# Cross-attention on one core: seven products for the first batch's output too, sums in PSUM taken at every stage, and the second batch's x in three places

## The chip, the cores and the metric

The kernel runs on one core of one Trainium2 chip, in fp32 throughout. The metric is the device time of one execution in microseconds. The profile comes from one further execution of the same program.

## The reference

Two batches of 2048 tokens with 640 channels attend with 20 heads of 32 channels to 77 text rows and 77 image rows of a context of 154 rows. Text and image have keys, values and softmax of their own; the two results are added.

```python
q = _split_heads(hidden_states @ Wq.T, H)
k = _split_heads(text @ Wk.T, H)
v = _split_heads(text @ Wv.T, H)
out_text = _merge_heads(_attend(q, k, v, sm_scale))
k_ip = _split_heads(ip @ Wk_ip.T, H)
v_ip = _split_heads(ip @ Wv_ip.T, H)
out_ip = _merge_heads(_attend(q, k_ip, v_ip, sm_scale))
out = out_text + IP_SCALE * out_ip
out = out @ Wo.T + bo
return out + residual
```

Here `_attend` is softmax(q k^T / sqrt(32)) v, IP_SCALE is 1, and the residual is x itself. All matrices lie in memory with the contracted dimension first, and the output is written with channels first.

## The kernel before

**Tiles.** The 640 channels are 5 row blocks of 128 (index c, four heads each; `NC`). A batch's 2048 tokens are 4 blocks of 512 (`TB`, index i) and two halves of 1024 (`sub`). The work is cut into 20 steps u: step u is pair q = u // 2 of batch and row block, and half sub = u % 2. Steps 0 to 9 are the first batch, 10 to 19 the second; step 20 is what is left of the attention.

**One step.** TensorE (PE) forms scores for 8 token tiles of 128 x 4 heads x 154 keys in three groups of 3, 3 and 2 tiles. Each group goes through a fixed sequence, and each of its members has a letter in the written orders, with the group's number behind it:

- R, `scores` (L216): TensorE, 32-row matmuls, in one half (four) of the eight PSUM banks.
- K, `take` (L228): ScalarE (ACT) copies the four banks into `pb`.
- M, `maxima` (L237): VectorE (DVE).
- S, `subtract` (L242): GpSimd (POOL).
- E, `exponential` (L248): ScalarE.
- D, `sums` (L255) and the reciprocals (L257): VectorE.
- N, `normalise` (L262): GpSimd.
- T, `transpose` (L269): VectorE, 32x32 blocks in place.

`pb` has three zones: odd steps share one, even steps take turns with the other two. In every even step, AT (`attend`, L278) multiplies the finished probabilities of the pair before with v for both halves, and CA (`take_attention`, L302 and L306) copies the result to `aT` on ScalarE.

**What fills TensorE beside it.** Items F0, F1, ... of a step are projections that need one bank each, and C0, C1, ... are the copies or takes of their results. `items_of` lists them: queries q of one 512-token block two or one steps ahead (`queries`, L184, five matmuls of 512 columns), keys k and values v of a row block (`project_kv`, L138, eight matmuls of 154 columns), and output chunks o and p. A chunk o is one row block by 512 tokens of the first batch's output, five matmuls (`Out.step`, L328); `Out.store` (L338) adds bias and residual on VectorE and stores. A chunk p is the last row block of the second batch's output without its last contraction block.

**After step 20.** The rest of the second batch's output (4 row blocks by 4 token blocks, contraction over 4 blocks) goes by Strassen's seven products: `group` handles two row blocks by two token blocks at a time, with products of 2 x 2 blocks (`product`, L430, two matmuls of 512 columns each), and the fifth contraction block added by `last_chunk` (L438). VectorE adds each product from PSUM to one or two sums in `pb` (`add`, L450 to L454). GpSimd forms the sums of weight blocks (`sum_w`, L386) and of token blocks (`sum_a`, L408) after the last N of step 19.

**The order.** The schedule is manual. `ORDERS` holds for each kind of step the half of the banks that R0, R1, R2 and AT use, the bank of each item, and the order of the work on TensorE, ScalarE, VectorE and GpSimd; a letter with a minus belongs to the step before. For a step of the first batch it reads:

```python
"even": (
    "1000", "547",
    "R0 R1 F1 R2 F2 F0 AT",
    "K0 K1 C1 K2 E0 E1 C2 E2 C0 CA",
    "C0 M0 M1 T1- C2 T2- C1 M2 D0 D1 D2 T0",
    "S0 S1 S2 N0 N1 N2",
),
```

Each engine runs its list strictly in that order and waits by semaphores for what an instruction reads or overwrites.

**Transfers.** All but a few of the first loads are issued by SP, in one queue in the order in which the program writes them; an entry that waits holds those behind it. `load_w` brings slices of the key and value weights into free slots in `aT`, `load_wq` the query weights of a row block (three places), `spread_v` copies v of a pair in 16 small transfers to four row groups, and `load_x` brings x in slices of 128 x 512. All four blocks of x of one batch stay in `xs`; the second batch's slices replace them in steps 6 to 9. `wo` is loaded in the second half of step 9, into the tile that held the context, after a first quarter of v's copies; then come the first three residuals.

Of the kernel before, what the change touches and what calls it, by code (L numbers as in the profile page):

```python
# [19 lines left out]
def kernel(  # L20
# [44 lines left out]
    NV = B * NHB * NC  # L65
    OPEN = 4
    FETCH = 3
# [4 lines left out]
    rpool = ctx.enter_context(tc.tile_pool(name="rpool", bufs=5))  # L72
# [9 lines left out]
    aT = const.tile([P, (NC + 1) * NHB, TB], F32, name="aT")  # L82

# [15 lines left out]
        aT[:, ds((NC - 1) * NHB + 2 * n, 2), :]  # L99
        .rearrange("p s t -> p (s t)")  # L100
        .rearrange("p (k o) -> p k o", k=NCC)
        for n in range(4)
# [47 lines left out]

    def spread_v(q):

        for g in range(G):
            for r in range(G):
                nc.sync.dma_start(
                    out=v4s[q % 2][r * D : (r + 1) * D, g].rearrange("p k d -> p (k d)"),
                    in_=squares(q)[g * D : (g + 1) * D],
                )
            if (q, g) == (NC - 1, 0):
                nc.sync.dma_start(out=wo, in_=WoT.rearrange("(c p) o -> p c o", p=P))  # L160
                for o in outs[:FETCH]:
                    o.fetch()
# [4 lines left out]
    def load_x():  # L167

        if slices:
            b, i, k = slices.pop(0)  # L170
            nc.sync.dma_start(out=xs[i][:, k], in_=xT[ts(k, P), ds(b * S + i * TB, TB)])
# [9 lines left out]
    def queries(u, h, pq):  # L181
        q, _, _, sub = step_of(u)
        for k in range(NC):
            nc.tensor.matmul(  # L184
                pq,
                wqs[q % 3][:, k, :],
                xs[sub * NH + h][:, k, :],
                start=(k == 0),
                stop=(k == NC - 1),
            )  # L190
# [95 lines left out]
    def rows_of_attention(b, c):  # L286


        if b == 0:
            return aT[:, ts(c, NHB)]  # L290
        if c == 0:
            return aT[:, ts(NC, NHB)]
        return aT[:, c - 1 : NHB * NHB : NHB]

    def take_attention(q, pa):
        b, c = divmod(q, NC)
        assert b == 0 or finished >= c * NC
# [11 lines left out]
    class Out:  # L309


        def __init__(self, v):
            self.v, self.n = v, len(outs)
            outs.append(self)
            self.b, r = divmod(v, NHB * NC)
            self.i, self.o = divmod(r, NC)
            self.tok = ds(self.b * S + self.i * TB, TB)
            self.res = self.po = None
            self.k = 0

        def fetch(self):

            if self.res is None:
                self.res = rpool.tile([P, TB], F32, tag="res", name=f"res_{self.v}")
                nc.sync.dma_start(out=self.res, in_=xT[ts(self.o, P), self.tok])

        def step(self):
            nc.tensor.matmul(  # L328
                self.po,
                wo[:, self.k, ts(self.o, P)],  # L330
                rows_of_attention(self.b, self.k)[:, self.i],
                start=(self.k == 0),
                stop=(self.k == NC - 1),
            )
            self.k += 1

        def store(self):
            nc.vector.scalar_tensor_tensor(  # L338
                self.res, self.po, bo_sb[:, self.o : self.o + 1], self.res, ALU.add, ALU.add
            )  # L340
            nc.sync.dma_start(out=outT[ts(self.o, P), self.tok], in_=self.res)
            for o in outs[self.n + 1 : self.n + 1 + FETCH]:
                o.fetch()


    outs = []
    for v in range(NV // B):
        Out(v)
    for i in range(NHB):
        Out(NV // B + i * NC + NC - 1)  # L350
    finished = 0
# [4 lines left out]
    PAIRS = ((0, 1), (2, 3))  # L356


    w_sums = xs[0].rearrange("p k t -> p (k t)").rearrange("p (n o) -> p n o", o=P)
    pb_flat = pb.rearrange("p z n g l -> p (z n g l)")  # L360
    pb_tiles = pb_flat.rearrange("p (n t) -> p n t", t=TB)
    a_sums = {(0, 0): xs[1], (0, 1): xs[2], (1, 0): xs[3], (1, 1): pb_tiles[:, :NC]}
    SUMS = (1, 4, 3, 7, 6)
    WSUMS = (1, 2, 5, 6, 7)

    def w_of(m, op, kp):

        (o1, o2), (k1, k2) = PAIRS[op], PAIRS[kp]
        blocks = [[wo[:, k, ts(o, P)] for k in (k1, k2)] for o in (o1, o2)]
        if m == 3:  # L370
            return blocks[0][0]
        if m == 4:
            return blocks[1][1]
        return w_sums[:, (op * 2 + kp) * len(WSUMS) + WSUMS.index(m)]

    def sum_w(op, kp, m):
        (o1, o2), (k1, k2) = PAIRS[op], PAIRS[kp]
        (a11, a12), (a21, a22) = [[wo[:, k, ts(o, P)] for k in (k1, k2)] for o in (o1, o2)]
        x, y, f = {
            1: (a11, a22, ALU.add),  # L380
            2: (a21, a22, ALU.add),
            5: (a11, a12, ALU.add),
            6: (a21, a11, ALU.subtract),
            7: (a12, a22, ALU.subtract),
        }[m]
        nc.gpsimd.tensor_tensor(w_of(m, op, kp), x, y, f)  # L386

    def blocks_of(ip, kp):
        return [[rows_of_attention(B - 1, k)[:, i] for i in PAIRS[ip]] for k in PAIRS[kp]]

    def a_of(m, ip, kp):
        if m == 2:
            return blocks_of(ip, kp)[0][0]
        if m == 5:
            return blocks_of(ip, kp)[1][1]
        return a_sums[(ip, kp)][:, SUMS.index(m)]

    def sum_a(ip, m):
        for kp in range(2):
            (b11, b12), (b21, b22) = blocks_of(ip, kp)  # L400
            x, y, f = {
                1: (b11, b22, ALU.add),
                3: (b12, b22, ALU.subtract),
                4: (b21, b11, ALU.subtract),
                6: (b11, b12, ALU.add),
                7: (b21, b22, ALU.add),
            }[m]
            nc.gpsimd.tensor_tensor(a_of(m, ip, kp), x, y, f)  # L408

    w_list = [(op, kp, m) for op in range(2) for kp in range(2) for m in WSUMS]  # L410

    def fetch_group(ip, op):
        for o in (1, 0):
            for i in range(2):
                nc.sync.dma_start(
                    out=sum_tile(ip, op, o, i),
                    in_=xT[ts(PAIRS[op][o], P), ds(S + PAIRS[ip][i] * TB, TB)],
                )

    def sum_tile(ip, op, o, i):  # L420
        return pb_tiles[:, NC + ((ip * 2 + op) * 2 + o) * 2 + i]

    def group(ip, op, bank_of):


        def product(m):
            ps = bank_of()
            own = {7: (0, 0), 6: (1, 1)}.get(m)
            for kp in range(2):
                nc.tensor.matmul(  # L430
                    ps, w_of(m, op, kp), a_of(m, ip, kp), start=(kp == 0), stop=(kp == 1 and not own)
                )
            if own:
                last_chunk(ps, *own, False)
            return ps

# [185 lines left out]
    def items_of(u):  # L622
# [3 lines left out]
        if u == NU:  # L626
            return [("p",)]
# [229 lines left out]
```

## Time and profile before

| | before |
|---|---|
| median of 3 runs | 515.19 us (514.83 to 515.55) |
| the profiled execution | 515.92 us |
| its span, first to last instruction | 514.1 us |
| TensorE busy | 504.6 us |
| VectorE busy | 398.4 us |
| GpSimd busy | 383.6 us |
| ScalarE busy | 242.9 us |
| moved by DMA | 52.03 MB, mean 101 GB/s |

The profile lists matmuls (PE) and weight loads (PEld) apart. An fp32 matmul shows as two records of each. Matmuls are pipelined, so the mean duration of a record is longer than the distance between two, and the distance is what a row of records costs. "Waits" are put down to the work that ended last before them.

### The profile page before, as it was taken

What the parts mean: (1) busy time and instruction counts of PE and PEld (TensorE: products, weight loads), DVE (VectorE), ACT (ScalarE), POOL (GpSimd) and SP (SyncE); (2) the same over time, 40 slices, a digit from 0 to 9 for tenths busy, and PEclk for the clock granted to TensorE, in tenths of its full rate; (3) what the DMA queues carried; (4) which work ended last, traced back from release to release, by engine and by line L of the source; (5) the groups of instructions that cost most, each with busy time, mean ns of one, the idle gap of its engine ahead of it and who ended that gap; (6) DMA issues with size and microseconds to landing.
All of it is one profiled execution on the core that took longest, in us unless ns stands there. A gap on an engine that the chain in (4) does not pass through costs nothing.

```text
span 514.1 us, 9615 instructions
## 1 busy us (share of the span) xinstructions
PE 504.6 (98%) x3998; PEld 271.0 (53%) x3998; DVE 398.4 (77%) x331; ACT 242.9 (47%) x421; POOL 383.6 (75%) x166
## 2 busy tenths in 40 slices
PE   8999999999999999999999999999999999999997
PEld 5657567567467565554454455444444544444442
DVE  0079899998989987988985898699887997176554
ACT  1175667666666556673564446546552760100000
POOL 0079999998998997789897688587796899991000
PEclk9999999999999999999999999999999999999999
DMA  8984321242164256211411220140111306254422
GB/s 250 355 224 120 97 68 47 61 112 62 50 210 145 58 174 205 55 48 29 137 40 43 77 72 1 42 131 18 43 38 44 100 15 182 76 172 143 143 82 82
DMA packets 54795, 52.03 MB, mean 101 GB/s; under 512 B 5728, under 2 KB 38752, under 8 KB 54752
## 3 DMA queue, kind: packets, MB, share of 16 engines
q1 hardware_dynamic: 54032, 51.09, 33.0%
q8 instruction: 31, 0.51, 0.4%
q10 hardware_dynamic: 720, 0.33, 0.2%
q14 instruction: 12, 0.10, 0.1%
HBM read 37.64 MB, written 10.49 MB: 94 GB/s over the span
## 4 chain that ended last, share of the span: by engine, by line
PE 93%; DMA 3%; ACT 1%; SPq 1%; DVE 1%; issue 0%; ACTq 0%
PE bank L184 32%; PE bank L328 20%; PE bank L278 11%; PE bank L216 10%; PE bank L430 9%; PE bank L138 8%; PE bank L438 3%; DMA aT<-in_L_xattn_Wk_ip_dram 2%; DMA x<-in_x_dram 1%; DMA wq<-in_L_xattn_Wq_dram 1%; SPq L492 1%; ACT pb L248 1%; DVE den L255 0%; ACT aT L302 0%; ACT pb L228 0%
## 5 line engine op out<-in xcount | busy, mean ns | idle before, releaser
L242 POOL TENSOR_TENSOR pb<-pb,mx 128x1848 f32<-128x1848 f32 (+1 forms) x60 | 175.6, 2943 | 71.1 <-DVE mx L237 70.8
L262 POOL TENSOR_TENSOR pb<-pb,rden 128x1848 f32<-128x1848 f32 (+1 forms) x60 | 175.0, 2942 | 10.1 <-DVE rden L257 8.4
L184 PE MATMUL bank<-x,wq 128*128 128x512 f32 x400 | 180.5, 601 | 1.1 <-ACT pb L228 0.7
L237 DVE TENSOR_REDUCE mx<-pb 128x24 f32<-128x1848 f32 (+1 forms) x60 | 109.4, 1845 | 50.7 <-ACT pb L228 50.7
L228 ACT COPY pb<-bank 128x462 f32<-128x462 f32 (+1 forms) x240 | 101.1, 541 | 54.2 <-PE bank L216 52.9
L184 PEld LDWEIGHTS bank<-x,wq 128*128 128x128 f32 x400 | 73.8, 191 | 89.2 <-issue 79.7
L255 DVE TENSOR_REDUCE den<-pb 128x24 f32<-128x1848 f32 (+1 forms) x60 | 110.3, 1838 | 12.5 <-ACT pb L248 12.2
L248 ACT ACTIVATE pb<-pb 128x1848 f32<-128x1848 f32 (+1 forms) x60 | 94.9, 1583 | 51.0 <-POOL pb L242 50.9
L269 DVE STREAM_TRANSPOSE pb<-pb 128x1920 f32<-128x1920 f32 (+1 forms) x60 | 114.7, 1927 | 2.4 <-POOL pb L262 2.4
L328 PE MATMUL bank<-aT,wo_ct 128*128 128x512 f32 x240 | 107.4, 599 | 0.0
L328 PEld LDWEIGHTS bank<-aT,wo_ct 128*128 128x128 f32 x240 | 44.3, 190 | 55.8 <-issue 52.6
L216 PEld LDWEIGHTS bank<-kT,qT 32*128 32x128 f32 x1280 | 48.4, 184 | 32.9 <-issue 28.6
L216 PE MATMUL bank<-kT,qT 32*128 32x154 f32 x1280 | 59.4, 307 | 2.1 <-DVE res L338 0.7
L278 PE MATMUL bank<-pb,v 32*32 32x512 f32 x1600 | 55.7, 597 | 1.0 <-issue 1.0
L194 ACT COPY qT<-bank 128x512 f32<-128x512 f32 x40 | 22.9, 585 | 53.1 <-PE bank L184 53.1
L138 PEld LDWEIGHTS bank<-wo_ct,aT 128*128 128x128 f32 x320 | 43.2, 188 | 4.9 <-issue 3.4
L138 PE MATMUL bank<-wo_ct,aT 128*128 128x154 f32 x320 | 44.9, 295 | 0.5 <-DMA aT<-in_L_xattn_Wk_ip_dram 0.5
L278 PEld LDWEIGHTS bank<-pb,v 32*32 32x32 f32 x1600 | 31.1, 103 | 20.2 <-issue 9.0
L338 DVE SCALAR_TENSOR_TENSOR res<-bank,bo_sb,res 128x512 f32<-128x512 f32 x24 | 16.9, 715 | 18.7 <-PE bank L328 16.6
L454 DVE TENSOR_TENSOR pb<-pb,bank 128x512 f32<-128x512 f32 x32 | 20.9, 685 | 10.7 <-PE bank L430 10.7
L306 ACT COPY aT<-bank 128x256 f32<-128x256 f32 x40 | 11.6, 406 | 21.1 <-PE bank L278 21.1
L450 DVE SCALAR_TENSOR_TENSOR pb<-bank,bo_sb,pb 128x512 f32<-128x512 f32 x16 | 11.6, 747 | 12.5 <-PE bank L438 12.5
(32 smaller groups left out, 180.3 us busy)
## 6 DMA issues: line engine op xcount, KB each, us to landing
x<-in_x_dram SPq DMA_DIRECT2D x40, 256.0 KB, 5.2
res<-in_x_dram SPq DMA_DIRECT2D x24, 256.0 KB, 3.4
out_dram<-res SPq DMA_DIRECT2D x24, 256.0 KB, 2.4
pb<-in_x_dram SPq DMA_DIRECT2D x16, 256.0 KB, 4.0
out_dram<-pb SPq DMA_DIRECT2D x16, 256.0 KB, 2.0
v<-vS SPq DMA_DIRECT2D x160, 20.0 KB, 1.8
wq<-in_L_xattn_Wq_dram SPq DMA_DIRECT2D x9, 320.0 KB, 4.7
aT<-in_L_xattn_Wk_dram SPq DMA_DIRECT2D x5, 512.0 KB, 4.5
```

Of the source, the lines that this page charges most:

```text
L138: nc.tensor.matmul(keys_in(out), loaded[n][:, k, :], cT[:, k, :, t, :], start=(k == 0), stop=(k == NCC - 1))
L184: nc.tensor.matmul(pq, wqs[q % 3][:, k, :], xs[sub * NH + h][:, k, :], start=(k == 0), stop=(k == NC - 1),)
L216: nc.tensor.matmul(ps[g][:, ts(t, 2 * L)], qTs[(u, h)][g * D : (g + 1) * D, ts(st, P)], kT[g * D : (g + 1) * D, c, b].rearrange("p t l -> ...
L228: nc.scalar.copy(keys_of(u, s)[:, :, g], ps[g][:, : n * 2 * L].rearrange("p (n l) -> p n l", n=n))
L237: nc.vector.tensor_reduce(mx, rows_of(u, s), AX.X, ALU.max)
L242: nc.gpsimd.tensor_tensor(rows_of(u, s), rows_of(u, s), maxs[s].unsqueeze(3).to_broadcast([P, n, 2, L]), ALU.subtract)
L248: nc.scalar.activation(e, e, AF.Exp, scale=SCALE)
L255: nc.vector.tensor_reduce(den, rows_of(u, s), AX.X, ALU.add)
L262: nc.gpsimd.tensor_tensor(rows_of(u, s), rows_of(u, s), rdens[s].unsqueeze(3).to_broadcast([P, n, 2, L]), ALU.mult)
L269: nc.vector.transpose(p, p)
L278: nc.tensor.matmul(pa[r][g * D : (g + 1) * D, :], v4s[q % 2][rows, g, k, :], zones[rows, :, g, k, :], start=(k == 0), stop=(k == NK - 1),)
L328: nc.tensor.matmul(self.po, wo[:, self.k, ts(self.o, P)], rows_of_attention(self.b, self.k)[:, self.i], start=(self.k == 0), stop=(self.k ...
```

## The change

The output of both batches is now formed by the same seven products, in another variant of the algorithm (four sums of weight blocks and four of token blocks in place of five and five, some built on others) and with other blocks: two by two sets of 128 rows and two halves of 256 tokens within one 512-token block, so that one product covers 2 x 128 rows by 256 tokens in one bank. `product` runs four matmuls of 256 columns, and two more for the fifth contraction block in products 2, 5, 3 and 4. The last row block of 128 stays in chunks of five matmuls of 512 columns (`last_chunk`).

Partial sums stay in PSUM: product 3 adds on the bank of product 5, 6 on that of 1, 7 on that of 6, and 4 on that of 7 (`JOINS`). After every product VectorE takes the bank into the sum of one quarter of the output (`take_product`): where a product is the first to reach its quarter, in two instructions of 256 columns with the bias, otherwise in one of 512. The sums of the first batch have one place (`acc`, with `res` for the last row block); each quarter is stored when it is complete, and the residual of the next 512 tokens is fetched into it one store later.

```diff
+    def product(m, b, i, ps):
+        fifth = {2: (0, 0), 5: (1, 1), 3: (None, 1), 4: (1, 0)}.get(m)
+        for op in range(2):
+            part = ps[:, ts(op, HT)]
             for kp in range(2):
                 nc.tensor.matmul(
-                    ps, w_of(m, op, kp), a_of(m, ip, kp), start=(kp == 0), stop=(kp == 1 and not own)
+                    part,
+                    w_of[m][:, kp, op],
+                    t_of(m, b, i)[:, kp],
+                    start=(op == kp == 0 and m in (1, 2, 5)),
...
+    def take_product(m, b, i, ps):
+        part = {2: (0, 0), 1: (0, 0), 5: (1, 1), 7: (1, 1), 3: (0, 1), 6: (0, 1), 4: (1, 0)}[m]
+        t = part_in(sums_of(b, i), *part)
+        if m in (5, 3, 4, 1 if b else 2):
+            for op in range(2):
+                bias = bo_sb[:, ds(2 * op + part[0], 1)]
+                nc.vector.scalar_tensor_tensor(
+                    t[:, op], ps[:, ts(op, HT)], bias, t[:, op], ALU.add, ALU.add
+                )
...
+        else:
+            nc.vector.tensor_tensor(t, t, ps.rearrange("p (op t) -> p op t", op=2), ALU.add)
```

The sums of the weights (`sum_w`, in two parts W0 and W1) and those of the first batch's tokens (`sum_t`, in the order as G1 to G4 for products 5, 6, 7 and 4) are GpSimd's, now in steps 10 to 19, written between its other work; the sums of the second batch's tokens follow the last N of step 19.

```diff
+    def sum_t(m, b, i):
+        x, y = {
+            5: (block(b, i, 0, 1), block(b, i, 0, 0)),
+            7: (block(b, i, 1, 1), block(b, i, 0, 1)),
+            6: (block(b, i, 1, 1), t_of(5, b, i)),
+            4: (block(b, i, 1, 0), t_of(6, b, i)),
         }[m]
-        nc.gpsimd.tensor_tensor(w_of(m, op, kp), x, y, f)
...
+        nc.gpsimd.tensor_tensor(t_of(m, b, i), x, y, ALU.subtract)
```

The weights' sums take the place of the fourth block of x. The second batch's x goes through the other three: each 512-token block of it is loaded again, as one transfer of 128 x 5 x 512, for each of the five row blocks, when the queries that last used the place have been issued. After each such load, what is left of v's copies is written (`spread_rest`). For the last pair of the first batch (step 9) the copies of v come in two halves, the second behind the load of x that waits for the first queries of step 9; `wo` follows the load of x that waits for the last queries of step 9, and the first residuals follow `wo`.

```diff
+    def load_next(u, h):
+        _, b, c, _ = step_of(u)
+        n = place_of(u, h)
+        if b == 0 and (c < NC - 1 or n == XROOM):
+            return
+        m = late.index((u, h)) + XROOM if b else n
+        if m < len(late):
+            v, g = late[m]
+            tokens = ds(S + (step_of(v)[3] * NH + g) * TB, TB)
+            nc.sync.dma_start(out=xs[n], in_=xT[:, tokens].rearrange("(k p) t -> p k t", p=P))
+            spread_rest()
```

The orders of all steps are written anew. Steps 10 to 19 have an order each, and what they do for the first batch's output is a table; "o1" is the last row block of token block 1, "21" product 2 of token block 1.

```diff
     ORDERS = {
         "0": (
-            "0111", "076",
-            "R2 R0 R1 F0 F2 F1",
-            "K2 K0 K1 E2 E0 C0 C2 E1 C1",
+            "1010", "430",
+            "R0 R1 R2 F2 F0 F1",
+            "K0 K1 K2 E0 E1 E2 C0 C2 C1",
...
         "10": (
+            "1001", "4110",
+            "F1 R0 R2 F0 R1 AT F2 F3",
+            "C1 K0 K2 C0 K1 CA E0 E2 E1",
+            "T2- T1- M0 M1 M2 D0 C2 C3 D1 D2 T0",
+            "G1 W0 S0 S2 S1 N0 W1 N1 N2",
+        ),
+        "11": (
+            "1100", "335421",
+            "R0 F1 R1 R2 F3 F2 F4 F0 F5",
+            "K0 C1 K1 K2 E0 C0 E1 E2",
+            "M0 C3 M1 M2 C4 T1- C2 D0 T2- D1 C5 D2 T0",
+            "S0 G2 S1 G3 S2 N0 N2 N1 G4",
+        ),
...
+    OUTPUT = {
+        10: "o0 20",
+        11: "10 50 30 60",
+        12: "70 40",
+        13: "o1 21 51 11",
+        14: "31 61",
+        15: "71 41 o2 22",
+        16: "52 12",
+        17: "32 62 72",
+        18: "42 o3 23",
+        19: "53 13 33 63 73 43",
     }
```

After step 20 the second batch's last row block and its 28 products follow in one written order, with one 512-token block's products mixed with the next one's.

## The prediction

> **What bounds the kernel now.** I read the engines' busy time and slices first, then the chain that ended last, then busy time by stage, then groups by shape, then the order of time around the places that the change moves.
>
> ```profile
> PE 504.6 (98%) x3998; PEld 271.0 (53%) x3998; DVE 398.4 (77%) x331; ACT 242.9 (47%) x421; POOL 383.6 (75%) x166
> ...
> PE 93%; DMA 3%; ACT 1%; SPq 1%; DVE 1%; issue 0%; ACTq 0%
> ```
>
> TensorE (PE) is busy 98% of the span and is 93% of the last chain. So TensorE's work is the time, and a wait elsewhere counts only where TensorE stands still for it. By stage (columns: length, then PE, PEld, DVE, ACT, POOL busy with instruction counts, granted clock, DMA share, GB/s):
>
> ```profile
> 76.27:113.37 37.10, 37.10 (x397) 23.39 (x396) 36.50 (x29) 24.65 (x44) 37.03 (x14) 1.00 0.28 76
> ...
> 315.85:362.03 46.18, 46.18 (x369) 22.63 (x369) 37.25 (x29) 23.66 (x40) 35.00 (x13) 1.00 0.17 54
> 362.03:408.93 46.90, 46.41 (x373) 22.33 (x372) 38.99 (x30) 23.18 (x42) 35.86 (x14) 1.00 0.21 60
> 408.93:441.48 32.55, 32.55 (x280) 15.74 (x279) 24.94 (x20) 11.73 (x21) 31.82 (x20) 1.00 0.32 88
> 441.48:510.40 68.92, 68.86 (x160) 30.25 (x160) 39.07 (x60) 1.95 (x8) 23.79 (x29) 1.00 0.36 122
> ```
>
> Each row but the last runs from one attention product (AT) to the next. A period of the first batch is 37.1 us, with VectorE and GpSimd busy 36.5 and 37.0 of it and TensorE still never idle. A period of the second batch is 46 us, with 37 and 35: about 10 us of room on each. The granted clock is 1.00 throughout.
>
> **The change part by part.** Prices of a matmul, from the chain in order of time (start, length, what):
>
> ```profile
> 36.55 2.11 PE bank L138 x16
> ...
> 243.92 8.58 PE bank L184 x20
> ...
> 254.24 4.49 PE bank L184 x10
> ```
>
> An fp32 matmul shows as two records (L184: 200 matmuls, 400 records). Twenty records of 512 columns take 8.58 us, 429 ns each, 0.858 us a matmul. Sixteen of 154 columns take 131.9 ns each. Ten that follow 32-row work (scores or AT) take 4.49 us, not 4.29: such a switch costs 0.2 us.
>
> *Fewer columns.* Before, the first batch's output is 20 chunks of 5 matmuls, 100. The second is 20 for its last row block and 4 groups of 18, 92. After, every 512 tokens of either batch take 5 matmuls of 512 columns, and 7 products of 4 with 4 x 2 fifth ones, 36 of 256 columns, worth 18: 23, in all 184 for 192. That is 8 x 0.858 = -6.86 us, all in the first batch's output, between AT of step 10 and AT of step 18.
>
> *Half-width matmuls.* 288 matmuls of 256 columns are 576 records in place of 288. No row has 256 columns. Between the two shapes measured the slope is (429 - 131.9)/358 = 0.830 ns a column, with 4.1 ns left per record. So 256 columns cost 216.6 ns, and 576 x 216.6 - 288 x 429 = +1.2 us. Weight loads do not bind: 154-column records already follow one another at 131.9 ns, each with its load. Against the change speaks the Trainium skill, TensorEngine Tiling (Array Packing), section Instruction Overhead: every matmul carries about 60 cycles of overhead. [...] that is 25 ns (an estimate), and 288 more records would cost 7.2 us and eat the whole gain. Taken on top of streaming, that doesn't fit the rows above, where a 154-column record would then need over 150 ns. I take 1.2 us, and keep 0.7 and 7.2 as ends.
>
> *Switches.* In the written order, 32-row work is followed by full matmuls 44 times before and 49 after: +1.0 us.
>
> *Opening.* Step 0 now runs R0 R1 R2 with R2 in the half of R0, so R2 waits for four score copies of 591 ns. Before, R1 waited for four of 443 behind the short R2. I place R2's end at 28.8 for 27.7 us; the next AT moves by +0.8 us. The rest of the first batch has the same matmuls and the same number of switches: 0, bounded by +-0.5.
>
> *Waits that lie in the old order.* The stages show 0.67 us (step 11 waits for VectorE's take of a bank), 0.49 (362 to 409), 0.32 (near 114), and R of step 19 takes 2.79 us for 48 records that stream in about 2.0. They go with the order: -2.2 us. What comes in their place: AT of step 10. Its last input now is the longer transpose:
>
> ```profile
> 210.98 5.71 DVE L269 STREAM_TRANSPOSE pb<-pb 128x1920 f32<-128x1920 f32 x3
> ...
> 216.94 5.52 PE L278 MATMUL bank<-pb,v 32*32 32x512 f32 x160
> ```
>
> The last transpose ends at 216.69 and AT starts at 216.94: no room. With group 1 (2.15 us) last instead of group 2 (1.49) TensorE waits about +0.5. After AT of step 20 only product 1 (1.7 us) stands before the last chunks that need its copies (before: a chunk of 3.4 us): +0.7.
>
> *GpSimd.* 16 sums of tokens (1.27 us each, L408) and the sums of the weights (W0 three and W1 one of 512 elements, one of 256: 5.8 us) now lie in the second batch's softmax, 26 us, where nothing of the kind lay before; at the end 20.3 us replace 34. Behind W0 stand S of step 10, then E on ScalarE, then the copies of step 11 that TensorE's R1 needs. W0 waits for Wo. SP issued Wo at 196.5, and it landed in 6.9 us. Now it stands behind the second half of v, and behind a load of x (1280 KB) that waits for the last queries of step 9, done near 205: issued at 207.5, and 2880 KB at Wo's own rate (1600 KB in 6.9 us) land at 220, at the 355 GB/s of the second slice at 216. I take 218. G1 ends at 216.4, W0 at 221.8; S of step 10 starts 3.7 us later than the old 218.1. Following the rows (S and N 3.29, 3.29, 2.25; E 1.75; W1 2; G2, G3 1.27), GpSimd ends N of step 11 at 261.8 and its last transpose ends at 264.0. TensorE reaches AT of step 12 at 217.4 + 5.5 + 43.8 = 266.7. Hidden with 2.5 us to spare; each us that Wo lands after 220.5 is a us lost. Later periods need 35.0 + about 4 of some 43 us.
>
> *VectorE.* A take of 256 columns is not in the trace: half of L338's 0.715 at least, 0.715 at most. The transposes (1280 in 1.486, 1920 in 2.148) give 1.03 ns an element, so about 0.19 of 0.715 is fixed: 0.45 us. Per 512 tokens 8 x 0.45 + 3 x 0.685 + 0.715 = 6.4 us for 5 x 0.715 = 3.6: +11 us over five periods, 39.5 of 43 us. These takes stand in VectorE's queue ahead of maxima and sums, and TensorE's next product on the same bank waits for them. A period of 37.1 with 36.5 shows that such a load can be hidden. I allow +0.5 us for all waits of this kind; bounds 0 and 3.5 for the first four periods.
>
> *Transfers.* x of the second batch is read once per row block: 20 loads of 1.31 MB for 5.2 MB in all, +21 MB. The stage ran at 54 GB/s; 5.2 MB more in a period of 43 us makes some 160. Each load is issued a whole three chunks (about 30 us) before its use and needs about 6. It stands on SP ahead of v's copies (16 x 0.64 us issue), stores and fetches of residuals. The tightest that I find is the fetch for part (0,0) of the third 512 tokens: it lands near 324.7, and VectorE wants it ahead of the maxima of step 15 near 325. 0 us; if 4 us late, GpSimd's 4.9 us of room in that period still covers it.
>
> *End.* The closing products have 76 matmuls' worth before and after; the last store hangs on two takes of 0.45 for one of 0.75: 0.
>
> Sum: -6.86 + 1.2 + 1.0 + 0.8 - 2.2 + 0.5 + 0.7 + 0.5 = -4.4 us. The profiled execution took 515.92 us (span 514.1 and 1.8 around it), 0.7 above the median of 515.19; I set the sum against the median: 510.8 us.
>
> **The rivals.** *One late start.* Wo or the weight sums come 3 to 5 us later than I placed them, R1 of step 11 and AT of step 12 wait, once: 512 to 514 us. For it: 0.25 us of room at AT of step 10, and Wo behind two transfers. Against: the 2.5 us that I count.
>
> *Softmax sets the period (slower).* VectorE, in order, stands at a take whose product TensorE hasn't reached; maxima, GpSimd's subtraction and so on slip, AT waits, and the next period starts late again. With 39.5 us of work on VectorE in 43, a loss of 1.5 us in each of the five periods is 7.5 us: about 518 us. It decides from 0.9 us a period on (4.4/5). For it: before, a second-batch period had some 9 us of idle VectorE; after 3. Against: the first batch's row, 36.5 of 37.1.
>
> *The page's price.* 25 ns per added record: 510.8 - 1.2 + 7.2 = 516.8 us. Against: both measured shapes.
>
> **How the numbers follow.** The likeliest, 510.8 (508.6 to 512.4; 508.6 with no new wait and the half-width cost at 0.7), has 0.70. One late start has 0.15, softmax as the bound 0.08, the page's price 0.03; 0.04 is left for what I don't see. 0.2%, about what a measurement of this kernel tells from no change, is 1.0 us: faster is below 514.2, slower above 516.2. Faster: 0.70 and most of 0.15, 0.85. Same: 0.06. Slower: 0.09. The range is 508.6 to 514.2: the likeliest and the late start, with slower cases left out.
>
> **What would show it.** Right: TensorE busy in all but some 8 us; 576 records of 256 columns near 217 ns apart; periods of 42 to 45 us in the second batch for 46 to 47; S of step 10 near 222; AT of step 18 about 6 us earlier than 403.5 and the closing products unchanged. Wrong: idle TensorE before an AT in every period, released by a transpose; a product that waits for VectorE's take; Wo landing after 221; half-width records spaced by 235 ns or more.

## The result, and the profile after

| | before | after |
|---|---|---|
| median of 4 runs each, side by side | 515.37 us (514.83 to 515.73) | 509.66 us (508.96 to 510.39) |
| span of the profiled execution | 514.1 us | 507.9 us |
| TensorE records | 3998 | 4270 |
| moved by DMA | 52.03 MB | 73.03 MB |

The ratio is 0.9894 with a 95% interval of 0.988 to 0.9907: 5.7 us faster, where 4.4 were forecast. Engines and chain shares of the profile after:

```profile
PE 498.6 (98%) x4270; PEld 320.2 (63%) x4270; DVE 392.0 (77%) x347; ACT 242.5 (48%) x421; POOL 395.1 (78%) x163
...
PE 84%; DMA 7%; POOL 4%; SPq 1%; DVE 1%; issue 1%; ACT 0%; DVEq 0%; POOLq 0%
```

TensorE does 6.0 us less work and still bounds the kernel. But its share of the chain fell from 93% to 84%, and 7% are now DMAs. The chain in order of time (start, length, what) shows which ones; here are its pieces from a load of x in step 9 to S of step 10:

```profile
199.30 6.54 DMA x<-in_x_dram
...
207.04 9.96 DMA wo_ct<-in_L_xattn_Wo_dram
217.16 1.29 POOL x L384
...
220.99 7.59 POOL pb L279 x3
```

Wo lands at 217.0, GpSimd's sums of weights W0 follow at once, and S of step 10 starts at 220.99. A piece of the chain need not have cost anything: TensorE worked beside it. What it cost shows only when it is moved. The second place of this kind is the fetch of a residual (chain, then VectorE in order of time with its idle time in brackets):

```profile
322.31 3.65 DMA acc<-in_x_dram
```

```profile
326.05 0.88 DVE L506 SCALAR_TENSOR_TENSOR acc<-bank,bo_sb,acc 128x256 f32<-128x256 f32 x2 [4.15 <-DMA acc<-in_x_dram]
```

VectorE stands still for 4.15 us, because the take of part (0,0) of the third 512 tokens wants that residual.

By stage, attention product to attention product, as the profile before was cut (length, PE, PEld, DVE, ACT, POOL, clock, DMA share, GB/s):

```profile
75.43:112.51 37.08, 37.08 (x396) 23.54 (x396) 34.84 (x27) 24.28 (x44) 34.89 (x13) 1.00 0.28 76
...
314.00:357.60 43.60, 42.77 (x385) 24.29 (x379) 38.26 (x32) 23.64 (x40) 38.83 (x16) 1.00 0.53 167
357.60:402.60 45.00, 45.00 (x404) 28.33 (x404) 41.10 (x39) 25.41 (x43) 42.56 (x18) 1.00 0.25 73
402.60:438.00 35.40, 35.40 (x316) 22.20 (x316) 28.47 (x26) 11.68 (x21) 34.40 (x18) 1.00 0.42 135
438.00:504.20 66.20, 65.86 (x298) 56.16 (x296) 24.32 (x46) 1.97 (x8) 12.00 (x10) 1.00 0.31 107
```

TensorE still works throughout in most stages. In the one from 314.0 it stands idle 0.83 us and, as e7 will show, loses more than that. With the starts of the attention products (AT) in both traces, and in the last version tried (e10), the time can be placed:

| from AT of step to AT of step | before | after | difference | e10 |
|---|---|---|---|---|
| 2 to 8 | 112.11 | 111.26 | -0.85 | 111.28 |
| 8 to 10 | 34.07 | 34.52 | +0.45 | 34.42 |
| 10 to 12 | 47.21 | 49.79 | +2.58 | 49.11 |
| 12 to 14 | 46.18 | 43.09 | -3.09 | 43.09 |
| 14 to 16 | 46.18 | 43.48 | -2.70 | 41.99 |
| 16 to 18 | 46.91 | 45.00 | -1.91 | 45.00 |
| 18 to 20 | 32.54 | 35.45 | +2.91 | 35.46 |
| 20 to TensorE's end | 74.39 | 71.72 | -2.67 | 71.71 |

Between AT of step 10 and AT of step 18 5.12 us are saved. The last two rows are mostly work that moved from behind AT of step 20 to ahead of it, +0.2 together. The table leaves out the 0.85 us up to AT of step 2 (70.76 to 69.91); they are taken up below.

### The profile page after: what moved, and what is told of

Its sections match the earlier page's. It is cut to its first block, busy times and chain, and to the rows that moved or that the text cites. A ratio compares the mean times of both kernels' runs of the same rounds, so it can differ in the third digit from the quotient of the medians.

```text
span 507.9 us, 10152 instructions
## 1 busy us (share of the span) xinstructions
PE 498.6 (98%) x4270; PEld 320.2 (63%) x4270; DVE 392.0 (77%) x347; ACT 242.5 (48%) x421; POOL 395.1 (78%) x163
## 2 busy tenths in 40 slices
DMA packets 71053, 73.03 MB, mean 144 GB/s; under 512 B 5600, under 2 KB 50912, under 8 KB 71008
## 4 chain that ended last, share of the span: by engine, by line
PE 84%; DMA 7%; POOL 4%; SPq 1%; DVE 1%; issue 1%; ACT 0%; DVEq 0%; POOLq 0%
PE bank L221 30%; PE bank L481 18%; PE bank L253 9%; PE bank L315 9%; PE bank L137 9%; PE bank L461 5%; PE bank L491 5%; DMA x<-in_x_dram 4%; DMA wo_ct<-in_L_xattn_Wo_dram 2%; POOL pb L299 2%; POOL pb L279 1%; SPq L175 1%; POOL x L384 1%; DMA acc<-in_x_dram 1%; DMA wq<-in_L_xattn_Wq_dram 1%
## 5 line engine op out<-in xcount | busy, mean ns | idle before, releaser
L253 PEld LDWEIGHTS bank<-kT,qT 32*128 32x128 f32 x1280 | 47.3, 184 | 26.8 <-issue 18.4
L481 PE MATMUL bank<-aT,wo_ct 128*128 128x256 f32 x192 | 47.6, 382 | 1.2 <-DVE acc L512 0.8
L481 PEld LDWEIGHTS bank<-aT,wo_ct 128*128 128x128 f32 x192 | 36.0, 190 | 11.1 <-issue 3.8
L461 PE MATMUL bank<-aT,wo_ct 128*128 128x512 f32 x80 | 36.1, 597 | 0.0
L506 DVE SCALAR_TENSOR_TENSOR pb<-bank,bo_sb,pb 128x256 f32<-128x256 f32 x24 | 10.5, 479 | 26.9 <-PE bank L491 16.4
L491 PE MATMUL bank<-aT,wo_ct 128*128 128x256 f32 x96 | 28.6, 379 | 0.0
L506 DVE SCALAR_TENSOR_TENSOR acc<-bank,bo_sb,acc 128x256 f32<-128x256 f32 x40 | 17.0, 468 | 13.5 <-PE bank L491 8.4
```

The source lines that it names most:

```text
L253: nc.tensor.matmul(ps[g][:, ts(t, 2 * L)], qTs[(u, h)][g * D : (g + 1) * D, ts(st, P)], kT[g * D : (g + 1) * D, c, b].rearrange("p t l -> ...
L481: nc.tensor.matmul(part, w_of[m][:, kp, op], t_of(m, b, i)[:, kp], start=(op == kp == 0 and m in (1, 2, 5)), stop=(op == 1 and kp == 1 and ...
```

## The experiments

My theory: the gain is the 8 x 512 columns, a half-width matmul costs about its columns, and the softmax of the second batch hides what was added to VectorE, GpSimd and SP. The rivals: a price per matmul, softmax as the bound, and a late start through Wo. Three runs cut the sum apart, three press on the covers, and the rest follow from what those showed. Differences to the kernel after are differences of medians; the two first-named kernels below start from the kernel before.

**e1, half width alone.** In the kernel before, every matmul of the output is two of 256 columns.

```diff
+    def halves_of(ps, w, t, first, last):
+        for h in range(2):
+            nc.tensor.matmul(ps[:, ts(h, TB // 2)], w, t[:, ts(h, TB // 2)], ...)
```

> The kernel before, with each of its 192 output matmuls of 512 columns cut into two of 256 columns with the same weights and the same sums; nothing else moves. If a record costs its streaming and 2 to 4 ns (the theory behind the prediction: 216 ns for 256 columns, 429 for 512), 768 records of 256 for 384 of 512 add 0.8 to 1.6 us: 516.2 to 517.0 us. If each added record costs 25 ns (the rule against the change), 384 more add 9.6 us: 525 us.

Measured: 516.54 us for 515.68, ratio 1.0019 (1.0008 to 1.0029). 192 matmuls more, 384 records, cost 1.0 us (0.0019 x 515.68): 2.6 ns a record, 1.1 to 3.9 by the interval. From AT of step 10 to TensorE's end, where all of them lie, the traces have 294.3 for 293.4 us. At the 25 ns a record that the prediction estimated it would have been 9.6 us more. The spacing in its closing products and in a run of products of the kernel after (both from the chain):

```profile
441.01 69.28 PE bank L311 x320
```

```profile
462.78 7.77 PE bank L481 x36
```

216.5 and 215.8 ns a record of 256 columns. The added matmul is paid by its columns and almost nothing else.

**e6, the first batch's orders alone.** The orders "0", "1", "even" and "odd" of the kernel after, put into the kernel before.

> The kernel before with the changed kernel's written orders for steps 0 to 7 (first step, second, even, odd) and all else as it was. In the two traces AT of step 10 starts at 215.7 for 216.9 us. If that is mainly the landing of the first weights (key scores start 0.84 us earlier before any order differs), the orders alone give -0.3 to +0.6 us (0.5 us lost at R of step 0, 0.3 us of waits gone): 515.1 to 516.0. If the orders brought it, 1.2 us are gone here too: 514.1.

Measured: 515.18 for 515.68 us, ratio 0.9993 (0.9979 to 1.0007), nothing that can be told from no change: the orders alone give between -1.1 and +0.4 us. The profiled execution, 517.93 us, was the slowest of 12 and says little of the orders. AT of step 8 to AT of step 10 took 36.27 us for 34.07 in it: 16 records of a key or value projection took 4.03 us for 2.37, because the granted clock (the column with 0.50) was halved for 3.4 us, and TensorE's stop at the end of AT of step 8, taken up in the last section, was 0.5 us longer.

```profile
190.90:194.30 3.40, 3.40 (x15) 3.40 (x15) 0.00 (x0) 0.00 (x0) 3.32 (x2) 0.50 0.00 0
```

What the orders give together with the rest, no run shows.

**e2, the columns back.** Product 2 of each of the first batch's 512 tokens runs its four matmuls of the four main blocks twice, 16 matmuls of 256 columns in all, as many columns as the change saved; its sum takes in the same terms twice.

```diff
-            for kp in range(2):
+            for again, kp in enumerate((0, 1, 0, 1) if b == 0 and m == 2 else (0, 1)):
```

> The changed kernel with as many columns put back as the change took out: product 2 of the first batch runs its four matmuls of the first four contraction blocks twice (so its sum is added twice), 16 matmuls of 256 columns more, in four places of steps 10 to 18. If TensorE's columns are the gain, they cost 16 x 2 x 0.216 = 6.9 us, less the 0 to 1 us by which TensorE waits there anyway: 515.6 to 516.6 us, the time of the kernel before. If that stage is set by the softmax on VectorE and GpSimd, or if the gain came from the new orders, they fill idle time and cost 3 us or less: below 513.

Measured: 516.16 us, ratio 1.002 (1.0005 to 1.0034), 6.5 us above the kernel after (6.2 in the traces, from the first score to TensorE's end). The columns are the gain.

**e3a and e3b, Wo later.** One or two loads of 1 MB (into `acc`, which the fetches then overwrite) stand ahead of Wo on SP.

```diff
             if w == "wo":
+                for _ in range(1):          # e3b: range(2)
+                    nc.sync.dma_start(out=acc, in_=xT[: (NC - 1) * P, :TB]...)
```

> The changed kernel with one more transfer of 1 MB (x into the place of the first batch's sums, overwritten by its own fetch later) ahead of Wo in SP's queue; nothing is left out. Wo lands 3 to 4 us later, near 221, and with it W0 and S of step 10. My working had 2.5 us to spare before AT of step 12 waits: then +0.5 to +1.5 us, 510.2 to 511.2. If the start of the second batch is already the limit, each us of delay is a us: 513 or more. If GpSimd has room there, 0.

> The same with two such transfers, the second waiting for the first: Wo lands some 9 us later, near 226. With 2.5 us to spare: +6 to +7 us, 516, all of it lost once, in steps 11 and 12. If GpSimd catches up within these steps: under +3 us.

Measured: 512.29 us, ratio 0.9939 (0.9924 to 0.9953), and 518.39 us, ratio 1.0054 (1.0039 to 1.0069): +2.6 and +8.7 over the kernel after. W0 started at 220.59 and 226.27 for 217.16, 3.4 and 9.1 us later; AT of step 10 to AT of step 12 took 53.42 and 58.58 for 49.79 us, 3.6 and 8.8 more. There was no room: a later Wo is paid from the first us. Where TensorE waits in e3a (TensorE in order of time):

```profile
235.40 3.42 PE L257 MATMUL bank<-kT,qT 32*128 32x154 f32 x40 [1.52 <-ACT pb L269]
```

These are R1 and R2 of step 11, behind R0 and a group of queries: 40 score records take 3.42 us for 1.59 in the kernel after, behind a wait of 1.52. They want banks that ScalarE has to copy, and ScalarE's copies stand in its queue behind E of step 10, which waits for S, which waits for W0:

```profile
233.17 1.75 ACT L289 ACTIVATE pb<-pb 128x1848 f32<-128x1848 f32 x1 [2.01 <-POOL pb L283]
234.82 1.86 ACT L269 COPY pb<-bank 128x462 f32<-128x462 f32 x4
```

In e3b the late Wo also stops the first output chunk itself, for 4.80 us. Part of what was measured is not Wo's but the clock's: in both traces the granted clock is halved at the wait, from 237.6 to 241.1 us in e3a and from 224.9 to 231.7 in e3b. In e3a:

```profile
237.60:241.10 3.50, 3.50 (x24) 2.74 (x17) 3.47 (x4) 3.14 (x8) 3.50 (x3) 0.51 0.65 156
```

The other three executions of e3a had the full clock and took 512.03 to 512.34 us, 2.4 to 2.7 more than the kernel after, so that a us of delay costs 0.7 to 0.8 us there. All four of e3b have a mean clock of 0.99; how much of its 8.7 us is the clock's, no run shows.

**e4, x of the second batch loaded into each of the three places once.** The other 17 of the 20 loads are left out, and the queries that wanted them use what lies there. It takes away the transfers' cost, all else standing.

```diff
-        if m < len(late):
+        if m < (len(late) if b == 0 else 0):
```

> The changed kernel without the 17 later loads of x: of the second batch only the first three token blocks are loaded, and later queries are formed from what lies in the three places (the sums are of other tokens; all instructions but these loads stay). 22 MB less are moved. If the traffic is hidden, as I counted it, the time falls by what the late residual and the late Wo cost, 0.8 to 1.3 us: 508.4 to 508.9. If 144 GB/s for 101 slows transfers that TensorE waits for, 3 us or more: below 507.

Measured: 506.18 us, ratio 0.9815 (0.98 to 0.983), 3.5 us below the kernel after. That is the price of the loads that I had put at 0. By stage: 1.57 us less from AT of step 8 to AT of step 10 (32.95 for 34.52), 0.69 from there to step 12 (49.10), 1.50 from step 14 to step 16 (41.98), the other stages the same within 0.02. Which transfer costs each was left to the next runs.

**e5a and e5b, VectorE's takes twice.** In the first batch, each of the 12 takes of 512 columns is done twice (e5a), or those and the 32 of 256 columns (e5b); the sums count these terms twice. That is 12 x 0.658 = 7.9 us more on VectorE, or 22.9 with 32 x 0.468. By groups of like shape, in the kernel after (count, busy us and mean ns, idle before; 3 and 8 of these takes are the second batch's):

```profile
L506 DVE SCALAR_TENSOR_TENSOR acc<-bank,bo_sb,acc 128x256 f32<-128x256 f32 x40 | 17.0, 468 | 13.5 <-PE bank L491 8.4 <-DMA acc<-in_x_dram 4.1 <-issue 0.8
...
L512 DVE TENSOR_TENSOR acc<-acc,bank 128x512 f32<-128x512 f32 x15 | 9.9, 658 | 3.6 <-PE bank L481 2.0 <-PE bank L491 1.7
```

> The changed kernel with only the 512-column takes of the first batch's products (1, 6, 7) done twice: 12 x 0.66 = 7.9 us more on VectorE over steps 10 to 19, 1.6 us a period (those sums are counted twice). With all takes twice, 22 us more on VectorE cost 12.3 us. If the cost begins where the room of some 3 us a period ends, under 1.5 us here: 509.7 to 511.2. If each take costs in proportion because the queue's order is what matters, 7.9/22 x 12.3 = 4.4 us: 514.

> The changed kernel with every take of the first batch's products done twice on VectorE (so these sums are counted twice, the residual once): about 22 us more work on VectorE in steps 10 to 19, 4.4 us in each period of some 43 us that held 39.5. If VectorE has the 3 us of room that I counted, each of four or five periods grows by 1 to 3 us: +5 to +12 us, 515 to 521. If the softmax already set the period, every us shows: +18 us or more. If it has much more room, under +3 us.

Measured: 512.78 us, ratio 0.9955 (0.9939 to 0.9971), and 521.96 us, ratio 1.0131 (1.0114 to 1.0148): +3.1 and +12.3. So on average VectorE's added work is paid at 0.4 to 0.5 us a us (3.1 / 7.9 and 12.3 / 22.9), although VectorE is busy only 38 of 43 us. The stages differ (what was added on VectorE, and how much longer the stage became than in the kernel after, in us):

| from AT of step to AT of step | e5a added | e5a longer | e5b added | e5b longer |
|---|---|---|---|---|
| 10 to 12 | 2.0 | 0.86 | 4.9 | 2.70 |
| 12 to 14 | 0.7 | 0 | 3.5 | 0.78 |
| 14 to 16 | 1.3 | 0.46 | 4.2 | 1.67 |
| 16 to 18 | 2.0 | 0.30 | 3.9 | 1.51 |
| 18 to 20 | 2.0 | 0.93 | 6.7 | 4.70 |

So there is some room, for most of what was added from 12 to 14 and for a third to a half of it from 18 to 20, and it does not show in the idle time of a stage. TensorE's waits in e5b, summed by releaser:

```profile
PE bank L481 <- DVE acc L513: 6.0, 6, 2.1
PE bank L253 <- DVE acc L506: 1.9, 3, 0.8
PE bank L481 <- DVE acc L506: 1.4, 1, 1.4
PE bank L315 <- DVE pb L306: 1.2, 1, 1.2
```

It waits for takes in many places, and for a transpose once. That is near the rival "softmax sets the period" (a bank waits for VectorE, whose queue holds other work first), though the rival told of an AT that waits, and that is seen once.

**e7, three places mended.** The rest of v's copies goes behind the fetch of the next residual on SP, in place of ahead of it; step 9's N and T are in another order, so that the short transpose is last ahead of AT of step 10; product 1 of the second 512 tokens stands before the last chunks after AT of step 20.

```diff
-        spread_rest(G * G // 2 if q == NC - 1 else None)
+        spread_rest(G * G // 2 if q >= NC - 1 else None)
...
             due[:] = [(i + 1, part)] if i + 1 < NHB else []
+            if i:
+                spread_rest()
...
-            "S0 S2 S1 N0 N2 N1",
+            "S0 S2 S1 N0 N1 N2",
...
-            "T2- T1- M0 M1 M2 D0 C2 C3 D1 D2 T0",
+            "T1- T2- M0 M1 M2 D0 C2 C3 D1 D2 T0",
```

> The changed kernel with three small moves against the waits that its trace shows: N of step 9 and its transposes end with the short group (TensorE waited 0.67 us before AT of step 10); v's copies of the second batch are written in two halves, the second behind a store and fetch (a residual landed at 326.0 and TensorE waited 0.82 us at 333); product 1 of the second token block is put before the last chunks (0.34 us behind AT of step 20). If these waits are the ones that end last, 1.0 to 1.8 us go: 507.9 to 508.7 us. If others lie close behind them, under 0.5 us goes: about 509.5.

Measured: 508.88 us, ratio 0.9868 (0.9856 to 0.9881), 0.8 below the kernel after. The fetch gives its 1.5 us (AT of step 14 to AT of step 16 in 41.98 us for 43.48). On SP, in the kernel after and then in e7:

```profile
309.09 12.55 SPq L175 DMA_DIRECT2D v<-vS  x16
321.74 0.53 SPq L452 DMA_DIRECT2D out_dram<-acc  x1
322.31 0.48 SPq L444 DMA_DIRECT2D acc<-in_x_dram  x1
```

```profile
309.89 7.50 SPq L175 DMA_DIRECT2D v<-vS  x8
317.57 0.44 SPq L452 DMA_DIRECT2D out_dram<-acc  x1
318.05 0.47 SPq L444 DMA_DIRECT2D acc<-in_x_dram  x1
```

The fetch stood behind 16 copies that took 12.55 us to issue, and is out 4.3 us earlier with 8. The order of step 9 made things worse: N1 waits 1.59 us for VectorE, and AT of step 10 waits 1.63 us for 0.67 (35.49 for 34.52 us from AT of step 8). As that AT came later and Wo did not, the stage behind it is shorter (49.10 for 49.79 us). Product 1 earlier changed nothing.

**e9, one load of x moved.** Near 176 the kernel after issues two loads of 1280 KB one behind the other. The second now goes out behind the first half of v's copies, at 196. The question was the stop of TensorE at the end of AT of step 8 that e4 did not have.

```diff
+            if m == XROOM:
+                held_back.append(load)
+                return
```

> The changed kernel with one load of x (1280 KB, the fourth of the second batch) moved on SP from right behind another such load, near 176 us, to behind the first half of v's copies, near 197. Both traces show TensorE stopping for 0.6 to 1.0 us at the end of AT of step 8 with nothing that it waits for, 1.5 us late in all, just after the DMA engines ran full for 4 to 6 us; without the later loads of x this stop was gone. If the two loads together cause it, 1.5 us go: 508.0 to 508.4 us. If it belongs to the place in the program and not to the transfers, nothing goes: 509.6.

Measured: 511.56 us, ratio 0.9931 (0.9917 to 0.9946), 1.9 above the kernel after. The stop was gone (AT of step 8 to AT of step 10 in 33.05 us for 34.52), but the moved load was wanted earlier than I had read, and it pushed Wo back:

```profile
203.03 4.56 PE L227 MATMUL bank<-x,wq 128*128 128x512 f32 x10 [0.56 <-DMA x<-in_x_dram]
```

```profile
219.01 1.29 POOL L390 TENSOR_TENSOR x<-wo_ct 128x512 f32<-128x512 f32 x1 [5.49 <-DMA wo_ct<-in_L_xattn_Wo_dram]
```

W0 at 219.01 against an AT of step 10 that came 1.0 us earlier is the case of e3a again, here at the full clock: W0 starts 4.32 us after that AT for 1.47, 2.85 us later, and AT of step 12 follows after 52.60 us for 49.79, 2.81 later.

**e8, e9's moved load with e7's fetch and product 1, and Wo ahead of that load.**

```diff
         if q == NC - 1:
+            nc.sync.dma_start(out=wo, in_=WoT.rearrange("(c p) o -> p c o", p=P))
+            for load in held_back:
+                nc.sync.dma_start(**load)
```

> The changed kernel with the load moved as above, Wo issued right behind the first half of v's copies (near 196 us for 207), the later copies of v in two halves around a store and fetch, and product 1 of the second token block ahead of the last chunks; all that without the change of order in step 9, which kept AT waiting longer. If the waits are independent, 1.5 + 0.7 + 1.4 + 0.3 = 3.9 us go: about 505.8 us. If GpSimd's added sums themselves hold step 11 (and not the late Wo), 0.7 less: 506.5.

Measured: 512.17 us, ratio 0.9941 (0.9925 to 0.9958). Now the load lands behind Wo, and TensorE waits for it ahead of its queries:

```profile
206.03 7.20 PE L227 MATMUL bank<-x,wq 128*128 128x512 f32 x10 [4.39 <-DMA x<-in_x_dram]
```

The ten records behind the wait take 7.20 us for 4.5, because the granted clock is halved from 204.5 to 211.4 us in this trace. AT of step 8 to AT of step 10 took 39.51 us. With Wo early and that AT late, AT of step 10 to AT of step 12 took 49.11 us.

**e10, what paid, and nothing else.** The kernel after with e7's order on SP for the fetch, and Wo issued behind the first half of v, with no load moved and step 9 as it was.

> The changed kernel with two of its issues on SP moved, nothing else: the stored parts of each 512 tokens drop the rest of v into SP's queue behind the fetches of residuals (as in e7), and Wo is issued right behind the first half of v, ahead of the load of x that is issued at 199.3 in the changed kernel. My theory: the fetches cost the changed kernel 1.5 us (AT of step 14 to AT of step 16 in 41.98 for 43.48 us, as e7 showed), Wo's landing 0.7 (AT of step 10 to AT of step 12 in 49.1 for 49.79, as e4 showed), and with step 9 in its old order nothing is lost ahead of AT of step 10: 509.7 - 2.2 = 507.4 us, GpSimd's first sum of weights directly behind its sums of tokens. Rival: Wo now stands before a load of x that TensorE wants at 209.5, and before the second half of v that AT of step 10 wants at 215.7; 1600 KB more ahead of them make TensorE wait there by 1 to 4 us, seen as an idle time released by the DMA of x or v, and the time is 509 to 512 us.

Measured: 507.88 us (507.51 to 509.52), ratio 0.9857 (0.9838 to 0.9876), 1.8 us below the kernel after where 2.2 were expected. It is the fastest of the kernels that compute everything. Fetch and Wo gave 1.49 and 0.68 us by the table above. The rival was half right: a wait for x did come, but where TensorE would have waited 0.67 us at AT of step 10 anyway:

```profile
210.35 4.53 PE L221 MATMUL bank<-x,wq 128*128 128x512 f32 x10 [1.11 <-DMA x<-in_x_dram]
```

W0 starts 2.7 us earlier than in the kernel after (214.44 for 217.16), for 0.68 us. Next to e3a, this sets the point from which Wo's landing decides: some 0.7 us earlier than the kernel after has it. From there on a us of delay costs 0.7 to 1.0 us (e3a's executions at the full clock, and e9).

## Why the prediction was right, and where its steps failed

The mechanism and the sign were right, and the time lies 1.1 us below the forecast 510.8. Step by step:

- *Fewer columns, -6.86.* Right: e2 gives 6.5 back.
- *Half-width matmuls, +1.2.* Right, a little dear: 576 x 215.8 ns - 288 x 429 ns = +0.75. e1 excludes the 7.2, which the prediction estimated from the Trainium skill, TensorEngine Tiling (Array Packing), section Instruction Overhead: about 60 cycles for each matmul, without a clock rate. For matmuls of 256 fp32 columns with full weights these are not added to the streaming. The page's next line, that one column takes as long as 60, makes them a floor, and a floor of 60 columns does not bear on 256.
- *Switches, +1.0.* Right. The price stands: ten records of 512 columns still take 4.49 us behind 32-row work and 4.29 otherwise. The count can be read in the order of the records in both traces: 44 before and 49 after, as told. No run tested it alone.
- *Opening, +0.8.* Mis-sized: 0. Scores of step 0 took 3.81 us for 3.30, as reasoned, but two waits of the old order near 57 and 59 us (0.38 and 0.23) went. From the scores of step 0 to AT of step 2 it is 46.27 us for 46.28. That AT came 0.85 us earlier because the scores began earlier (23.64 for 24.48): no step of mine, and no effect of the change. In the ten other kernels that start from the one after they begin at 23.29 to 24.48 us, and in e1, whose first steps are those of the kernel before, at 23.57.
- *Waits of the old order, -2.2.* Too small: -3.3. A group of 16, 24, 40 or 48 score records takes 0.74, 1.00, 1.74 or 1.78 us where nothing holds it. In the kernel before, four groups took longer: 24 near 113 us 1.83, 40 near 227 us 2.71, 40 near 366 us 2.21, and 48 near 409 us 2.79, and these losses are gone. I had gone by idle times (0.32, 0.67, 0.49), which leave out what a group loses between its records, and had taken 2.0 us for the usual length of the 48 of step 19. The usual length of 48, and that one (both from the chain before):

```profile
132.25 1.78 PE bank L216 x48
```

```profile
408.93 2.79 PE bank L216 x48
```

- *AT of step 10, +0.5; after AT of step 20, +0.7.* 0.67 and 0.34; AT of step 8 to AT of step 10 as a whole is 0.45 longer. The other order of N and T, which I had thought of as the better one, was worse (e7).
- *VectorE's takes, +0.5.* The 0.45 us for a take of 256 columns was 0.468, and VectorE has the idle time that I counted on (38.3 busy in the 43.6 us from 314.0, where I reckoned with 39.5 of 43). The term itself came to nothing. TensorE's waits near products are 0.18, 0.46 and 0.82 us, and the last two went away in e10 with Wo and the fetch. In e10 every stage from AT of step 10 to AT of step 20 takes, within 0.03 us, what its records and switches cost at the figures of this part, with 5.45 us for AT. So idle time did cover the takes of this change, as I had thought, but where more is added (e5a and e5b) part of it is paid at once in most stages.
- *Wo "hidden with 2.5 us to spare".* This step failed. The landing was right (217.0 for the 218 I took; S of step 10 at 220.99 for 222). But I followed the work to AT of step 12 alone. The chain that I had named myself, E on ScalarE and behind it the copies that step 11's scores want, ends some 30 us earlier, and there the room was less than nothing, 0.7 us.
- *Transfers, 0.* Failed: e4 gives 3.5 back. 1.5 are the fetch, and "if 4 us late, GpSimd's 4.9 us of room still covers it" is the step that failed: it landed at 325.96, VectorE was free for it at 321.9, and the take held back the maxima that stood behind it; of the 4.15 us on VectorE 1.5 came through to TensorE, with 4.8 us of idle GpSimd in the period. 0.7 are Wo's, and 1.5 the stop at AT of step 8 (which the kernel before has as well, so that it is not a cost of the change).
- *Told signs.* Periods of 43 to 45 us came for 46 to 47, except the first, which took 49.79 us for 47.21; in e10, with Wo earlier, it still takes 49.11, since more products lie in it. AT of step 18 started at 397.05, 6.4 us earlier, where 6 were told. Of the signs of being wrong one came: a product waited 0.82 us for VectorE's take, near 333 us, behind the late fetch.

With the measured sizes the sum is -6.86 + 0.75 + 1.0 + 0 - 3.3 + 0.45 (AT of step 10) + 0.34 + 0 + 0.7 (Wo) + 1.5 (fetch) = -5.4 us, against -5.7 between the medians. With the first scores, which began 0.84 us earlier in the profiled execution, it is -6.3, against -6.2 between the spans. That the total was close is partly luck: two costs put at nothing (Wo and the fetch, 2.2) stood against old waits larger than I had read (1.1) and costs that came smaller or not at all (opening, takes, half-width matmuls and the time after AT of step 20, 2.1).

## What to carry to other kernels

On an engine that works in order, the idle time of a stage does not tell how much more fits in it: follow a late piece to the first instruction that stands behind it on any queue, not to the end of the stage, and delay it on purpose to see what it costs. A fetch that follows a store belonged ahead of bulk copies in the same queue here, for 1.5 us. Halving a matmul's columns to halve the block of a fast product cost 2.6 ns a record here, so a scheme that saves columns can be cut fine. Before a stage of one trace is explained, look at the clock that was granted in it.

## What was not expected of the hardware

**A stop for want of instructions.** TensorE stops at the end of AT of step 8 for no reason that the profile names, in the kernel before and after alike (after, then before; TensorE in order of time):

```profile
181.17 5.50 PE L315 MATMUL bank<-pb,v 32*32 32x512 f32 x158
187.25 1.01 PE L315 MATMUL bank<-pb,v 32*32 32x512 f32 x2 [0.58 <-issue]
```

```profile
182.87 5.50 PE L278 MATMUL bank<-pb,v 32*32 32x512 f32 x159
189.38 0.58 PE L278 MATMUL bank<-pb,v 32*32 32x512 f32 x1 [1.01 <-issue]
```

The product ends 7.0 us after its start, where it takes 5.5 elsewhere: 1.5 us. Just before it the DMA engines run full; the kernel after and then e4, which has no stop there, in the same 2 us (last column GB/s):

```profile
182.00:184.00 2.00, 2.00 (x82) 1.21 (x67) 2.00 (x1) 1.87 (x3) 1.29 (x1) 1.00 1.06 397
```

```profile
182.00:184.00 2.00, 2.00 (x77) 1.16 (x65) 2.00 (x1) 1.88 (x3) 1.35 (x1) 1.00 0.04 8
```

In e4, e8 and e9, with one of the two large loads at that time, the stop is gone. What TensorE lacks can be read from one DMA queue, q8, of the kind "instruction". Its blocks are of 16 KB (before, then after; number, MB, share of the span):

```profile
q8 instruction: 31, 0.51, 0.4%
```

```profile
q8 instruction: 33, 0.54, 0.5%
```

There are 31 before, 33 after and 34 in e1, one for about every 258 of TensorE's matmul records and weight loads, so they are taken here for TensorE's own instructions. The block that is due in AT of step 8, in us:

| kernel | AT starts | block sets out | block has landed | stop ends |
|---|---|---|---|---|
| before | 182.87 | 186.86 | 187.92 | 189.38 |
| after | 181.17 | 184.67 | 185.71 | 187.25 |
| e10 | 181.39 | 184.51 | 185.56 | 187.12 |
| e4 | 181.24 | 182.39 | 183.75 | no stop |
| e8 | 180.82 | 181.96 | 183.39 | no stop |
| e9 | 181.64 | 182.76 | 184.00 | no stop |

With one large load the block sets out 1.1 to 1.2 us after the start of AT. In the other eleven kernels, which load more of x at that time, it does so 3.1 to 4.2 us after it. In the 14 traces TensorE has 15 idle times of over 0.1 us that are put down to "issue", and each ends 1.3 to 1.6 us after such a block landed. The 0.32 us near 114 in the kernel before is one of them; others lie in AT of step 12 in e2 and in AT of step 18 in e6. So the loads delay TensorE's next instructions, and it runs out of them. No semaphore in a trace says so: it is read from these times.

**A wait that halves the clock.** In ten of the 14 traces the granted clock is 1.00 from 7 us on until TensorE's last matmul. In the other four it is 0.5 for a while, at or behind a wait: for 6.8 us in e3b (a wait of 4.80 us) and e8 (4.39 us), and for 3.4 us in e3a (1.52 us) and e6 (behind the stop, 1.09 us, with TensorE busy for 2.31 of the 3.4 us ahead of the fall). Such a wait costs more than its length: in e8 the ten records behind it took 2.7 us longer than usual.
